# Routing moved within the experts' pipeline, and attention's batches reordered and interleaved

## The chip, the cores and the metric

The kernel runs on one core of one Trainium2 chip. A NeuronCore has TensorE (PE, the matrix engine), VectorE (DVE), ScalarE (ACT), GpSimd (POOL) and SyncE (SP), which mostly issues transfers. Each executes its own instructions in order, and they wait for one another through semaphores. The metric is device time in microseconds of one execution, lower is better.

## The reference

The input is x, 4 batches of 1024 tokens of width 256. Four layers are added to it, each on a layernorm of x: a selective state space layer, an FFN, a linear attention, and the same FFN with the same weights again.

```python
x = x + ssm(layernorm(x))
x = x + ffn(layernorm(x))
x = x + attention(layernorm(x))
x = x + ffn(layernorm(x))

def attention(x):                          # 16 heads of 16, no mask, batches independent
    q, k = relu(x @ Wq) / 4, relu(x @ Wk) / 4
    v, u = x @ Wv, silu(x @ Wu)
    kv  = einsum('bhlk,bhlv->bhkv', k, v)
    out = einsum('bhlk,bhkv->bhlv', q, kv)
    return (srms_norm(out) * u) @ Wo

def ffn(x):
    queries = (x @ W_q).reshape(2, n, 64)   # n = 4096 tokens
    scores  = two top-8 lists against 64 keys each, 64 pair sums, top-8 of these
    ew      = silu(x . down_embed[idx]) * softmax(scores)
    return (silu(x @ gate_w) * (x @ up_w)) @ down_w + sum(ew * up_embed[idx])
```

The first half of the query rows meets the first set of keys and the second half the second, so the routing of tokens of group g needs the queries of group g // 2 and of group g // 2 + 4. A group is 512 tokens; there are 8 groups, two per batch.

## The kernel before

Everything is float32. The tokens are handled in groups of 512 on tiles of 128 partitions.

**State space layer** (`ssm`, lines 112 to 813). It loops over groups and state indices with hand-written order. All its calls go through `Pinned`, which keeps program order. Beside its scan run queues of small stages: `ends` (the layer's output, and a layernorm whose transpose goes to DRAM as `hs[g]`) and `mlps` (the dense half of the first FFN for a group, whose result goes to DRAM as `xs[g]`; `stored` says for which groups). Each stage is announced with its cost in PE time.

**Experts' pipeline** (`experts`, from line 1144 on). When the scan is over, this runs the routed half of the first FFN, still in program order on the pinned engines. The loop has 8 steps per group: `g, k = step // 8, step % 8`. In it:

- `queries` computes qT for two groups in steps k = 0, 1, 2 of odd groups.
- `begin(g + 1)` creates the generator `route` for the next group and runs its first part, eight small matmuls into the one bank named `route`. The rest of `route` is written one part per step by `next(routes[g], None)`: the copy to `r` on ACT, eight times `max` and `max_index` on DVE (tiles `v`, `iu`), the pair sums and their top-8 (`d`, `pv`, `sc`, `left`), counts and normalisation (`cnt`, `zi`, `last`), then `most`, `ex`, the table `tb` on POOL, `code` and `eq`, then `rank`, then a comparison into `eq`, and `tb` multiplied by it. The four DVE operations on 2048 elements (`eq`, `rank`, `eq`, `tb`) take some 2.3 us each.
- `apply(g)` begins at k = 2 and takes 14 steps: four products `emb` with a silu into `wt`, transposes of `tb` into `st` (two banks), the weighing of `wt` by `st` on DVE, the products `up` into `o` (two banks), and the sums `raised` of `x` and `o` on DVE.
- `beside(cost)` lets waiting stages of `ends` and `mlps` run on the PE: `left` is raised by a constant each step, capped at 6.0, and lowered by `COST[k]`, the PE time of the step's own work.

Since the engines are in order, what is written first in a step is also executed first. In a step before the change the part of `route` is written ahead of the parts of `apply`.

**Attention** (`attention`, lines 817 to 937). Here the engines are not pinned: a scheduler of the framework orders the instructions on each engine, from the program order, the dependencies and the buffers. A batch is a pass of `for b in range(B)`: layernorm and transposes of its two groups into `hT`; eight times the products for k, v and gate, evacuated to `kk` (ACT), `vv` (DVE) and `u` (ACT), and the accumulation in two banks `kv`; the query products to `qT` (ACT); the masked `kvb`; eight output products `po`, each copied to `o` (DVE), squared to `sq` (ACT) and reduced to `oss` (DVE); square root (ACT), reciprocal, `u * o` (POOL), the scaling into `o` (DVE); transposes to `oT`, the products with `Wo`, and the sums into `x`. The PSUM pools are `at_mm` (four banks), `at_kv` (two) and `at_o` (two, shared by gate, `po` and `Wo` products). `u` and `o` have one buffer, the other tiles two.

**Last FFN** (`ffn`, lines 1323 to 1371). Layernorm, transposes and queries of the groups in the order 0, 4, 1, 5, 2, 6, 3, 7, then a loop over groups with the routing of the next group beside the dense products. It takes all parts of `route` in one go.

Of the kernel before, what the change touches and what calls it, by code (L numbers as in the profile page):

```python
# [12 lines left out]
F32 = mybir.dt.float32  # L13
# [38 lines left out]
class Net:  # L52
# [764 lines left out]
    def attention(self):  # L817
        nc, tc = self.nc, self.tc
        with ExitStack() as ctx:
            wp = ctx.enter_context(tc.tile_pool(name="at_w", bufs=1, reuse_waits="tile"))  # L820
            one = ctx.enter_context(tc.tile_pool(name="at_one", bufs=1, reuse_waits="tile"))
            two = ctx.enter_context(tc.tile_pool(name="at_two", bufs=2, reuse_waits="tile"))
            mm = ctx.enter_context(tc.tile_pool(name="at_mm", bufs=4, space=PSUM, reuse_waits="tile"))
            kvp = ctx.enter_context(tc.tile_pool(name="at_kv", bufs=1, space=PSUM, reuse_waits="tile"))
# [22 lines left out]
            scale = 1.0 / DH**0.5  # L847
            BT = L // P

            for b in range(B):  # L850
                groups = (2 * b, 2 * b + 1)
                hT = two.tile([P, KD, L], F32, tag="hT", name="hT")
                for i, g in enumerate(groups):
                    ln = two.tile([P, TG, D], F32, tag="ln", name="ln")
                    self.layernorm(g, ln)
                    for k in range(KD):
                        ps = self.transposed(mm, ln, k)
                        nc.vector.tensor_copy(hT[:, k, i * G : (i + 1) * G], ps)
                kv = [
                    kvp.tile([P, P], F32, tag=f"kv{c}", name=f"kv{c}") for c in range(KD)  # L860
                ]
                u = one.tile([P, BT, D], F32, tag="u", name="u")
                for t in range(BT):
                    ts = slice(t * P, (t + 1) * P)
                    ps = self.product(mm, [(hT[:, k, ts], wkv[:, k, :]) for k in range(KD)])
                    kk = two.tile([P, D], F32, tag="kk", name="kk")
                    nc.scalar.activation(kk, ps[:, :D], AF.Relu, scale=scale)
                    vv = two.tile([P, D], F32, tag="vv", name="vv")
                    nc.vector.tensor_copy(vv, ps[:, D:])
                    for c in range(KD):  # L870
                        nc.tensor.matmul(
                            kv[c], lhsT=kk[:, c * P : (c + 1) * P],
                            rhs=vv[:, c * P : (c + 1) * P], start=t == 0, stop=t == BT - 1,
                        )
                    ps = self.product(
                        op, [(hT[:, k, ts], wu[:, k, :]) for k in range(KD)], n=D, tag="o"
                    )
                    nc.scalar.activation(u[:, t, :], ps, AF.Silu)
                qT = two.tile([P, KD, L], F32, tag="qT", name="qT")
                for c in range(KD):  # L880
                    for i in range(L // G):
                        ps = self.product(
                            mm,
                            [
                                (wq[:, k, c * P : (c + 1) * P], hT[:, k, i * G : (i + 1) * G])
                                for k in range(KD)
                            ],
                        )
                        nc.scalar.activation(
                            qT[:, c, i * G : (i + 1) * G], ps, AF.Relu, scale=scale  # L890
                        )
                kvb = two.tile([P, KD, P], F32, tag="kvb", name="kvb")
                for c in range(KD):
                    nc.vector.tensor_tensor(kvb[:, c, :], kv[c], mask, ALU.mult)
                o = one.tile([P, BT, D], F32, tag="o", name="o")
                ss = two.tile([P, BT, HEADS], F32, tag="oss", name="oss")
                for t in range(BT):
                    po = op.tile([P, D], F32, tag="o", name="po")
                    for c in range(KD):
                        nc.tensor.matmul(  # L900
                            po[:, c * P : (c + 1) * P],
                            lhsT=qT[:, c, t * P : (t + 1) * P], rhs=kvb[:, c, :],
                            start=True, stop=True,
                        )
                    nc.vector.tensor_copy(o[:, t, :], po)
                    sq = two.tile([P, D], F32, tag="sq", name="sq")
                    nc.scalar.activation(sq, po, AF.Square, scale=1.0 / DH**0.5)
                    nc.vector.tensor_reduce(
                        ss[:, t, :], sq.rearrange("p (h d) -> p h d", d=DH), AX.X, ALU.add
                    )  # L910

                nc.vector.tensor_scalar(ss, ss, 1e-24, None, ALU.max)
                rt = two.tile([P, BT, HEADS], F32, tag="ort", name="ort")
                nc.scalar.activation(rt, ss, AF.Sqrt)
                nc.vector.reciprocal(ss, rt)
                for t in range(BT):
                    nc.gpsimd.tensor_tensor(u[:, t, :], u[:, t, :], o[:, t, :], ALU.mult)
                    nc.vector.tensor_tensor(
                        o[:, t, :].rearrange("p (h d) -> p h d", d=DH),
                        u[:, t, :].rearrange("p (h d) -> p h d", d=DH),  # L920
                        ss[:, t, :].unsqueeze(2).to_broadcast([P, HEADS, DH]),
                        ALU.mult,
                    )
                for i, g in enumerate(groups):
                    oT = two.tile([P, KD, G], F32, tag="oT", name="oT")
                    for k in range(KD):
                        ps = self.transposed(mm, o[:, i * TG : (i + 1) * TG, :], k)
                        nc.scalar.copy(oT[:, k, :], ps)
                    for t in range(TG):
                        ps = self.product(  # L930
                            op,
                            [(oT[:, k, t * P : (t + 1) * P], wo[:, k, :]) for k in range(KD)],
                            n=D, tag="o",
                        )
                        nc.vector.tensor_tensor(
                            self.x[g][:, t, :], self.x[g][:, t, :], ps, ALU.add
                        )


    def expert_weights(self, pool):  # L940
# [27 lines left out]
    def route(self, nc, w, g, qT, pools, got):  # L968
# [21 lines left out]
        v = sm.tile([P, 2 * M4, TOPK], F32, tag="v", name="v")  # L990
        iu = sm.tile([P, 2 * M4, TOPK], U32, tag="iu", name="iu")
        for i in range(2 * M4):
            nc.vector.max(v[:, i, :], r[:, i, :])
            nc.vector.max_index(iu[:, i, :], v[:, i, :], r[:, i, :])
        yield
# [148 lines left out]
    def experts(self, w, xpool, xs, hs, rest):  # L1144
# [3 lines left out]
        with ExitStack() as ctx:  # L1148
# [121 lines left out]
                yield  # L1270

            left = [0.0]
            COST = (0.9, 0.9, 1.7, 3.4, 3.4, 1.7, 1.7, 2.7)

            def beside(cost):
                left[0] = min(left[0] + 3.6, 6.0) - cost
                for q in (ends, mlps):
                    c = q.next_cost()
                    if c is not None and c[0] <= left[0]:
                        q.stage()  # L1280
                        left[0] -= c[0]
# [5 lines left out]
            for _ in range(3):  # L1287
                next(asked)
                beside(1.7)
            begin(0)  # L1290
            load(hT, 0)
            applied = []
            for step in range(8 * NG + 6):
                g, k = step // 8, step % 8
                if k == 0 and g < NG:
                    while g not in rest.stored:
                        ends.stage()
                        mlps.stage()
                    self.x[g] = xpool.tile([P, TG, D], F32, tag=f"x{g}", name=f"x{g}")
                    nc.sync.dma_start(out=self.x[g], in_=xs[g])  # L1300
                if g < NG:
                    next(routes[g], None)
                if k == 2 and g < NG:
                    applied.append(apply(g))
                for a in list(applied):
                    if next(a, self) is self:
                        applied.remove(a)
                if g + 1 < NG:
                    if k == 0 and g % 2:
                        asked = queries((g + 1) // 2)  # L1310
                    if k < 3 and g % 2:
                        next(asked)
                    if k == 7:
                        begin(g + 1)

                    if k == 5 and g % 2 == 0 and g + 2 < NG:
                        load(asks, (g + 2) // 2)
                        load(asks, (g + 2) // 2 + half)
                    if k == 6:
                        load(hT, g + 1)  # L1320
                beside(COST[k] + (1.7 if g % 2 and k < 2 else 0))

# [120 lines left out]
```

## Time and profile before

| what | value |
|---|---|
| median of 3 runs | 2202.4 us (2200.65 to 2205.84) |
| the profiled execution | 2205.35 us, span 2203.6 us |
| TensorE | 1923.9 us busy (87%), mean granted clock 0.951 |
| VectorE | 1591.7 us busy (72%) |
| ScalarE, GpSimd | 1020.0 us (46%), 1029.5 us (47%) |
| experts' pipeline | about 1204 to 1473 us |
| attention | about 1473 to 1697 us |
| last FFN | about 1697 us to the end |

Busy time is the union of an engine's instructions. A line L47 stands for everything that goes through `Pinned`, and L106 for all products made by the helper `product`, so such work is told apart by its tiles: `out<-in` names what is written and read. In a timeline a row begins with its start and its length in us, and ends in brackets with the time that the engine stood idle before it and what ended that. One matmul of the program in float32 shows as two or more rows of the profile.

### The profile page before, as it was taken

How to read it: one execution, taken by the hardware profiler on the slowest of the kernel's cores; microseconds unless marked ns; L12 is line 12 of the kernel's file. 1: busy time of each engine (PE TensorE's matmuls, PEld its weight loads, DVE VectorE, ACT ScalarE, POOL GpSimd, SP SyncE). 2: the span in 40 equal slices, each digit the busy share in tenths (PEclk: the TensorE clock that was granted, in tenths of full speed). 3: DMA queues.
4: the chain of work that ended last, by engine and by line, in shares of the span. 5: the costliest groups of instructions: out<-in, count | busy, mean ns of one | idle time of the engine just before them, and what ended most of it. 6: DMA issues, size and time to landing. Idle time of an engine off the chain costs nothing.

```text
span 2203.6 us, 22814 instructions
## 1 busy us (share of the span) xinstructions
PE 1923.9 (87%) x7712; PEld 1215.5 (55%) x7712; DVE 1591.7 (72%) x2843; ACT 1020.0 (46%) x1557; POOL 1029.5 (47%) x691
## 2 busy tenths in 40 slices
PE   6586888989889899799878898878888899999999
PEld 2334545656556556456554555556665466666665
DVE  2798988969989889798897888874445555555551
ACT  2465686766767767767645242213332311111111
POOL 2559778687787877878875214211111000000000
PEclk9797999999999999999989999989999999999999
DMA  2311212222122221222113032020000000000000
GB/s 72 97 54 39 68 51 75 62 81 70 62 78 58 71 77 61 82 72 63 53 60 117 19 115 77 29 82 0 1 0 1 1 10 10 10 10 10 10 9 11
DMA packets 84757, 106.13 MB, mean 48 GB/s; under 512 B 7840, under 2 KB 53920, under 8 KB 84640
## 3 DMA queue, kind: packets, MB, share of 16 engines
q1 hardware_dynamic: 78064, 98.00, 14.4%
q10 hardware_dynamic: 6576, 6.67, 0.9%
q8 instruction: 61, 1.00, 0.2%
q14 instruction: 56, 0.46, 0.1%
HBM read 90.75 MB, written 13.89 MB: 47 GB/s over the span
## 4 chain that ended last, share of the span: by engine, by line
PE 56%; DVE 20%; ACT 11%; issue 6%; POOL 4%; DMA 2%; ACTq 0%; SPq 0%; DVEq 0%; POOLq 0%
PE ps L106 22%; PE hT L47 5%; DVE h L47 4%; PE conv L47 4%; DVE acc L47 4%; PE gate L47 3%; PE up L47 3%; ACT L47 3%; ACT a L47 3%; PE xin L47 2%; PE down L47 2%; PE out L47 2%; PE emb L47 2%; PE dt L47 2%; PE o L47 2%
## 5 line engine op out<-in xcount | busy, mean ns | idle before, releaser
L47 POOL TENSOR_TENSOR u<-dx,bt 128x1024 f32<-128x1024 f32 x256 | 603.7, 2366 | 264.9 <-DVE h L47 133.7
L47 PE MATMUL hT<-ident,h 128*128 128x128 f32 x2048 | 305.6, 290 | 120.3 <-DVE acc L47 118.0
L47 DVE SCALAR_TENSOR_TENSOR acc<-hT,cT,acc 128x512 f32<-128x512 f32 x512 | 355.8, 736 | 40.6 <-PE hT L47 39.7
L47 ACT ACTIVATE a<-delta,a_neg 128x512 f32<-128x512 f32 x512 | 340.1, 688 | 92.1 <-DVE h L47 72.0
L47 PEld LDWEIGHTS hT<-ident,h 128*128 128x128 f32 x2048 | 247.2, 148 | 245.3 <-DVE acc L47 194.3
L47 DVE TENSOR_TENSOR_SCAN h<-a,state,u 128x512 f32<-128x512 f32 x256 | 314.9, 1267 | 38.6 <-ACT a L47 37.5
L47 DVE TENSOR_TENSOR_SCAN h<-a,u 128x512 f32<-128x512 f32 x256 | 299.4, 1206 | 59.3 <-ACT a L47 54.6
L1068 POOL TENSOR_TENSOR tb<-ex,d 128x2048 f32<-128x2048 f32 x8 | 29.1, 3641 | 400.8 <-PE ps L106 370.3
L1365 DVE TENSOR_TENSOR act<-s,ps 128x512 f32<-128x512 f32 x64 | 43.8, 685 | 145.3 <-PE ps L106 145.3
L1363 ACT ACTIVATE s<-ps 128x512 f32<-128x512 f32 x64 | 38.2, 597 | 229.5 <-PE ps L106 222.3
L47 ACT ACT_TABLE_LOAD x92 | 118.0, 1283 | 45.8 <-DVE d L47 22.9
L47 PE MATMUL up<-hT,up_w 128*128 128x512 f32 x256 | 123.8, 609 | 7.7 <-DMA up_w<-in_up_w 6.5
L47 PE MATMUL down<-w_down_w,av 128*128 128x256 f32 x512 | 121.2, 382 | 9.3 <-DVE xw L47 7.9
L47 PE MATMUL gate<-hT,gate_w 128*128 128x512 f32 x256 | 122.3, 610 | 5.5 <-DMA gate_w<-in_gate_w 5.5
L106 PE MATMUL ps<-hT,w_gate_w 128*128 128x512 f32 x256 | 121.5, 597 | 4.3 <-DVE act L1365 4.3
L106 PE MATMUL ps<-hT,w_up_w 128*128 128x512 f32 x256 | 120.9, 595 | 0.0
L106 PE MATMUL ps<-w_down_w,act 128*128 128x256 f32 x512 | 116.6, 380 | 3.9 <-DVE x L1140 3.9
L47 POOL TENSOR_TENSOR tb<-ex,d 128x2048 f32<-128x2048 f32 x8 | 45.9, 5742 | 145.6 <-DVE code L47 145.6
L47 PEld LDWEIGHTS down<-w_down_w,av 128*128 128x128 f32 x512 | 95.4, 191 | 32.0 <-issue 9.7
L106 PEld LDWEIGHTS ps<-w_down_w,act 128*128 128x128 f32 x512 | 96.0, 190 | 22.1 <-DVE x L1140 9.7
L47 PE MATMUL conv<-xin,taps 128*128 128x512 f32 x224 | 104.8, 595 | 1.5 <-ACT xc L47 1.5
L47 POOL TENSOR_TENSOR av<-av,up_v 128x512 f32<-128x512 f32 x64 | 82.4, 1291 | 14.2 <-ACT up_v L47 14.2
(250 smaller groups left out, 3280.8 us busy)
## 6 DMA issues: line engine op xcount, KB each, us to landing
bt<-bcd SPq DMA_DIRECT2D x128, 256.0 KB, 3.3
gate_w<-in_gate_w SPq DMA_DIRECT2D x64, 128.0 KB, 3.0
up_w<-in_up_w SPq DMA_DIRECT2D x64, 128.0 KB, 2.5
hT<-hs SPq DMA_DIRECT2D x16, 512.0 KB, 4.3
taps<-conv_d SPq DMA_DIRECT2D x28, 256.0 KB, 3.7
xw<-in_x SPq DMA_DIRECT2D x8, 512.0 KB, 4.4
in_wT<-in_in_wT SPq DMA_DIRECT2D x8, 512.0 KB, 4.6
skip_wT<-in_skip_wT SPq DMA_DIRECT2D x8, 512.0 KB, 4.7
```

The lines of the kernel that those rows point to most:

```text
L47: return self.tc.keep_in_program_order(f(*args, **kw))
L106: self.nc.tensor.matmul(ps, lhsT=lhsT, rhs=rhs, start=i == 0, stop=i == len(pairs) - 1)
L1068: nc.gpsimd.tensor_tensor(tbv, ex.unsqueeze(3).to_broadcast(sht), d[:, M4:, 0:NKEY].unsqueeze(2).to_broadcast(sht), ALU.mult,)
L1363: nc.scalar.activation(s, pg, AF.Silu)
L1365: nc.vector.tensor_tensor(a, s, pu, ALU.mult)
```

## The change

In the experts' pipeline:

- In a step, the part of the next group's routing is now written after the parts of `apply`, so behind its sums and weighings.
- `begin(g + 1)` moves from k = 7 to k = 5, and at k = 6 the next part, the copy to `r`, is written as well. For group 0 both are written ahead of the loop.
- The eight `max` and `max_index` are split by a further `yield` into four and four, at k = 0 and k = 1. The later parts keep their steps.
- `COST` exchanges its entries for k = 5 and k = 7, and `left` is raised by 3.5 in place of 3.6 per step.

In attention the body of the loop becomes the generator `batch(b)` with two `yield`s: ahead of the masked `kvb`, and after the last `oss`. The batches are taken in the order 0, 2, 1, 3. The output part of a batch (up to `oss`) is written first, then the first part of the next batch (up to `qT`), then the last part of the former (norm, gating, `Wo`, sums). `u` and `o` get two buffers and the pool `at_one` goes.

`route` is shared with the last FFN, which takes all its parts at once; the further `yield` changes nothing there.

```diff
@@ attention
-            one = ctx.enter_context(tc.tile_pool(name="at_one", bufs=1, reuse_waits="tile"))
...
-            for b in range(B):
+            def batch(b):
                 groups = (2 * b, 2 * b + 1)
...
-                u = one.tile([P, BT, D], F32, tag="u", name="u")
+                u = two.tile([P, BT, D], F32, tag="u", name="u")
...
+                yield
                 kvb = two.tile([P, KD, P], F32, tag="kvb", name="kvb")
...
-                o = one.tile([P, BT, D], F32, tag="o", name="o")
+                o = two.tile([P, BT, D], F32, tag="o", name="o")
...
+                yield
 
                 nc.vector.tensor_scalar(ss, ss, 1e-24, None, ALU.max)
...
+            order = [batch(b) for b in (0, 2, 1, 3)]
+            next(order[0])
+            for i, now in enumerate(order):
+                next(now)
+                if i + 1 < B:
+                    next(order[i + 1])
+                next(now, None)
@@ route
         for i in range(2 * M4):
+            if i == M4:
+                yield
             nc.vector.max(v[:, i, :], r[:, i, :])
             nc.vector.max_index(iu[:, i, :], v[:, i, :], r[:, i, :])
@@ experts
-            COST = (0.9, 0.9, 1.7, 3.4, 3.4, 1.7, 1.7, 2.7)
+            COST = (0.9, 0.9, 1.7, 3.4, 3.4, 2.7, 1.7, 1.7)
 
             def beside(cost):
-                left[0] = min(left[0] + 3.6, 6.0) - cost
+                left[0] = min(left[0] + 3.5, 6.0) - cost
...
             begin(0)
+            next(routes[0])
             load(hT, 0)
...
-                if g < NG:
-                    next(routes[g], None)
                 if k == 2 and g < NG:
                     applied.append(apply(g))
                 for a in list(applied):
                     if next(a, self) is self:
                         applied.remove(a)
+                if g < NG:
+                    next(routes[g], None)
...
-                    if k == 7:
+                    if k == 5:
                         begin(g + 1)
+                    if k == 6:
+                        next(routes[g + 1])
```

## The prediction

> **What bounds the kernel now.** I read the page first for the stages, then busy time by stretches, then the waits of TensorE (PE) and VectorE (DVE) in the two stages the diff touches, then the timeline around the longest of them.
>
> The page (40 slices of 55 us): DVE is at 6 to 9 tenths up to about 1487 us and at 4 or 5 after it; the PE clock row has an 8 in the slice from 1432 to 1487 us, where the PE pauses.
>
> ```profile
> span 2203.6 us, 22814 instructions
> ...
> DVE  2798988969989889798897888874445555555551
> ...
> PEclk9797999999999999999989999989999999999999
> ```
>
> Busy time of three stretches (columns: length, then busy time with instruction counts for PE, PE weight loads, DVE, ACT, POOL, then PE clock, DMA share, GB/s): experts' pipeline, attention, last FFN.
>
> ```profile
> 1200.00:1472.00 272.00, 230.87 (x866) 152.59 (x866) 221.38 (x644) 70.22 (x99) 70.78 (x33) 0.94 0.21 72
> 1472.00:1697.00 225.00, 199.04 (x837) 135.78 (x835) 102.36 (x281) 65.63 (x139) 28.78 (x39) 0.93 0.03 9
> 1697.00:2204.00 507.00, 490.50 (x1696) 300.98 (x1696) 257.44 (x677) 98.70 (x145) 33.35 (x12) 1.00 0.03 9
> ```
>
> In the experts' stage PE and DVE are both some 80% busy: neither is the bound alone, each waits for the other. In attention only the PE is loaded. The last FFN is PE work at full clock, and its order hardly changes.
>
> Who waits in the experts' stage from its first top-8 on (columns: total us, times, longest):
>
> ```profile
> PE o L47 <- DVE x L47: 21.1, 7, 5.0
> PE st L47 <- DVE wt L47: 12.0, 7, 4.2
> ...
> DVE v L47 <- ACT r L47: 14.8, 5, 4.3
> DVE xw L47 <- PE down L47: 9.6, 4, 5.0
> DVE x L47 <- PE o L47: 7.7, 8, 1.5
> ```
>
> The timeline shows why:
>
> ```profile
> 1419.29 2.29 DVE L47 TENSOR_TENSOR eq<-iota,code 128x2048 f32<-128x2048 f32 x1
> ...
> 1421.50 0.74 DVE L47 TENSOR_TENSOR x<-x,o 128x256 f32<-128x256 f32 x2
> 1421.96 5.72 PE L47 MATMUL o<-w_up_emb,wt 128*128 128x256 f32 x16 [5.02 <-DVE x L47]
> ```
>
> The PE's third output product needs one of the two `o` banks, which the sum `x` frees. The sum takes 0.42 us, but on DVE it stands behind the next group's routing, `eq` last. After the 5.02 us gap 16 matmuls take 5.72 us instead of 3.6.
>
> In attention, per batch:
>
> ```profile
> 1519.90 2.33 PE L97 MATMUL tr<-ident,o 128*128 128x128 f32 x9 [4.13 <-DVE o L918]
> ...
> 1522.06 5.17 PE L106 MATMUL ps<-w_Wo,oT 128*128 128x256 f32 x16
> ```
>
> The PE idles 4.13 us through norm, square root and gating of a batch, then runs slowly.
>
> **What the Trainium skill says.** "TensorE: Matmul & The Clock Gate", Part 1: a PE idle for about 3.4 us falls to half clock and needs about as long busy to return. The trace agrees: after 5.02 us idle 16 matmuls lose 2.1 us, and clocks of 0.83 and 0.87 stand in the two most broken group stretches. "Perfetto Trace Analysis", Identifying Performance Opportunities: where the most contended engine changes between regimes, interleave them. It fits: attention's projections leave DVE idle, its output part leaves the PE idle. "ScalarE: Activation LUTs", What ACT_TABLE_LOAD costs: 1283 ns per load and about 1380 ns of drain. The trace shows loads of 1.28 us; the drain has no row of its own.
>
> **The change, part by part.** All savings are from the profiled execution, 2205.35 us (span 2203.6), which is 2.95 above the median of 2202.4; I subtract savings from the median.
>
> *Attention.* Instructions are the same, apart from order and doubled `u` and `o`. A batch repeats every 54.75 us (1530.31 to 1585.06). Its PE work at gapless rates: key/value/gate loop 8 x 3.03 = 24.2 (steps at 1546.58, 1549.60), query products 16 x 0.43 = 6.9, `po` 32 x 0.108 = 3.4, two sets of 16 transposes at 0.11 = 3.5, `Wo` 32 x 0.215 = 6.9. Sum 44.9, so 9.9 us a batch is lost: 4.1 for `o`, 1.6 for `sq` (four gaps of about 0.5 between `po` pairs), 2.8 slow clock (9 transposes 2.33 against 1.0; 16 `Wo` 5.17 against 3.7), 1.4 in small ones. The changed program's PE order puts the next batch's LN transposes and first projections between `po` pairs, and the previous batch's `Wo` after the next batch's query products. So three of the four losses go; the last batch's output part has nothing beside it and keeps its own.
>
> What stays: I laid the new order out with the durations above. `po` pairs still wait for copy (0.42) plus square (0.42) of the pair before, with 5 and 10 transposes (0.55, 1.1) between: about 1.6 us a transition with the `vv` copies now behind `ln` and `oss` on DVE. Each moved `Wo` block waits for two 0.59 us ACT copies behind the last `qT` copy, twice: 1.6. In the later transitions `po`, `Wo` and the gate products share two banks: 0.9 more each. Kept: 3 x 1.6 + 3 x 1.6 + 2 x 0.9 = 11.4. Saved 29.7 - 11.4 = **18 us** (12 to 25). The two table loads (2 x 1.28, or 5.3 with the skill's drain) now stand in the next batch's loop: `kk` and `u` behind them are late by 3 to 5 us once; four `mm` banks cover the first. I take 0 and keep 6 us over three batches as the bad end, and below zero nothing, since ACT gains no idle time here.
>
> *Experts: routing behind the sums, and begun at k = 5.* DVE work is unchanged; `r` now exists two steps ahead of its top-8. Measured by groups (first top-8 to the next; the last to the last sum): 24.65, 34.50, 31.36, 31.16, 33.28, 32.93, 29.75, 38.97, together 256.6. The busier of PE and DVE in each: 22.97, 29.05, 27.55, 28.70, 30.52, 30.86, 25.76, 34.14, together 229.6. The rest, 27 us or 3.4 a group, is mutual waiting. In the changed order I count PE products and DVE operations by group at the same durations: busier engine 23.0, 29.3, 26.3, 28.3, 26.6, 28.4, 28.6, 31.2, together 221.7. The 8 us come from the PE pieces of the MLPs being spread later (rate 3.5 for 3.6: the last `down` products now lie beside group 6's weighing), and 3 us of `ln` moved out of the tail.
>
> Waiting does not vanish: `v<-r` goes (14.8 less the 3.25 of the first), and of `o<-x` and `st<-wt` I expect half, as sums and weighings now precede the long routing operations, but sums wait for `up` products that stand behind MLP pieces. I take 2.2 a group, 17.6: stage 239.3, **17 us** less. Ends: 3.4 a group gives 8, 1 a group gives 27.
>
> Moved steps on other queues: the routing's 8 small matmuls (0.9 us) go two steps earlier on PE, ahead of two `emb` products; the `r` copy (0.59) precedes two silus on ACT, which idles most of the stage; the POOL table product (5.74) keeps its step; on SP the loads of `hs` and `x` keep their number, and the `gate_w`/`up_w` loads move by a step. I cost these at nothing: ACT (70 of 272) and DMA (0.21) hide them.
>
> *Junction.* The first `ln` of attention now follows the last `x` sum on DVE, where before it lay inside the tail. Four `ln` (0.34 each), four transposes and two `hT` copies (0.69) put the first projection 3.5 to 4 us after the last sum; before it was 3.4 (1473.42 to 1476.81), because it waited for the `Wv` load (2.10). I take 1 us lost (0 to 3).
>
> Sum: 18 + 17 - 1 = 34; 2205.35 - 34 = 2171 for a profiled run, **2168 us** against the median.
>
> **Rivals.**
> 1. Only attention gains: the sums now wait for PE products, so mutual waiting stays above 4 us a group and eats the regrouping. 2202 - 18 = 2184. For it: `x<-o` already waits 8 times; against: those are short, 1.5 at most.
> 2. Both nearly ideal: waits of 1 a group, attention keeps 5 instead of 11. 27 + 25 - 1 = 51, 2151. Against: two `op` banks and one in-order DVE.
> 3. Only the experts' stage gains: the doubled tiles and new order stall on ACT's table loads and `Wo` copies, returning the 18. 2202 - 16 = 2186. Against: ACT is busy 66 of 225 there.
> 4. Slower: DVE blocks at the sums. At k = 4 `raised` waits on DVE for two `up` products, and the whole routing queues behind it, then the table, then the next group's transposes. The wait is the PE's time from weighing to sum (`emb` 1.7, `up` 3.4, plus MLP pieces of 1.7 each) less DVE's cover (3.5 + 3.9 for top-8 and counts). It is zero up to one piece and 1.7 for each more; cancelling 34 us over 8 groups needs 4.3 us more a group, three pieces beyond that one. The budget (3.5 a step, capped at 6.0, less the step's own work) leaves about two. With four pieces: 8 x 5.1 + 3 = 44 lost against 34 gained, 2212.
> 5. The change doesn't do what it says, since attention's order is a scheduler's: the built order shows it moved, so only a few per cent.
>
> **How the numbers follow.** Likeliest 0.62 at 2168 (own range 2158 to 2178); rival 1 0.13; rival 3 0.08; rival 2 0.10; rivals 4 and 5 0.07, split 0.05 slower and 0.02 within. The 80% range, 2150 to 2190, takes in rivals 1 to 3 and the bounds above. A measurement can tell about 0.2% (4.4 us) from no change: faster 0.92 (the first four less 0.01 for their edges), same 0.03, slower 0.05.
>
> **What would show it.** Right: `v<-r` gone from DVE's waits; `o<-x` on PE at half or less; group spacing of the table products near 29; the 4.13 us waits before `tr<-ident,o` only once, in the last batch; attention near 207 us; the last FFN at 507. Wrong: new DVE waits `x<-o` above 2 us, PE waits on `u` or `kk` after a table load, or an experts' stage above 265.

## The result, and the profile after

The changed kernel took 2167.52 us in the median of six runs (2166.62 to 2179.4), the kernel before 2203.03 (2200.06 to 2205.84) beside it: a ratio of 0.9847, 95% interval 0.9822 to 0.9873. The forecast was 2168. The profiled execution took 2167.88 us.

Executions of one kernel lie up to 18 us apart (of the six here four lie near 2167 and two near 2178), and most of that is there when the scan ends, before any changed instruction (its last `acc` ended between 1198.2 and 1214.8 us in the traces below); so stages are compared from there on, and whole times by their ratios.

The page of the changed kernel: span, busy tenths of VectorE, and the PE's clock. DVE's heavy part ends in the same slice as before, the 27th, but a slice is now 54.2 us long in place of 55.1, so that it ends at about 1462 us in place of 1487. The 8 in the clock row, in the tail of the experts' stage, is still there.

```profile
span 2166.2 us, 22802 instructions
...
DVE  2798998978989979888798789984446545555551
...
PEclk9798999999999999999999999989999999999999
```

Busy time by stretches of the changed kernel (length, then PE, weight loads, DVE, ACT, POOL with counts, PE clock, DMA share, GB/s): experts' stage, attention, last FFN.

```profile
1200.00:1459.00 259.00, 228.19 (x864) 152.27 (x864) 223.29 (x628) 70.53 (x99) 71.45 (x31) 0.93 0.24 79
1459.00:1658.20 199.20, 190.32 (x832) 129.03 (x833) 101.15 (x298) 64.67 (x139) 30.92 (x40) 0.98 0.02 5
1658.20:2166.20 508.00, 492.04 (x1696) 301.73 (x1696) 257.17 (x676) 98.69 (x145) 33.33 (x12) 0.99 0.03 9
```

DVE's busy time is within 2 us of what it was in each stretch, and so is the PE's in the last FFN. In attention the PE is busy 8.7 us less (190.32 for 199.04), with its clock at 0.98 in place of 0.93, and idle 9 us in place of 26. In the experts' stage it is busy 2.7 us less, and the clock is no better (0.93 for 0.94): what shrank there is idle time.

The changed kernel's waits of PE, then of DVE, from the end of the scan to the last experts' sum (total us, times, longest):

```profile
PE st L47 <- DVE bnmv L83: 6.9, 1, 6.9
PE o L47 <- DVE x L47: 6.3, 3, 3.2
...
PE st L47 <- DVE wt L47: 3.5, 3, 1.7
```

```profile
DVE x L47 <- PE o L47: 12.8, 9, 4.1
DVE v L47 <- ACT r L47: 11.4, 1, 11.4
```

The waits for `x` and `wt` fell to a third, and `v<-r` is left only ahead of the first top-8. Others grew: the sums wait longer for `o` (12.8 us for 8.5, each in nine waits; the 7.7 of the prediction leaves out the last one), the PE waits 3.6 us for a `gate_w` transfer where it was 0.7, and it stands still for 6.9 us once, at a wait put down to `bnmv`, a layernorm statistic of attention. What stands still there are the transposes `st`, which read the table `tb`:

```profile
1417.90 1.94 PE L47 MATMUL st<-ident,tb 128*128 128x128 f32 x8 [6.90 <-DVE bnmv L83]
```

The last long operation on `tb` ended at 1417.76 us on DVE, and the statistic, 0.17 us long, stands directly behind it. So this is a wait for the table, under the name of its neighbour.

In attention, PE's waits in the changed kernel:

```profile
PE tr L97 <- DVE o L919: 4.1, 1, 4.1
PE tr L97 <- DVE ln L88: 1.9, 2, 1.1
...
PE po L900 <- ACT sq L907: 0.4, 2, 0.2
PE ps L106 <- ACT oT L929: 0.2, 1, 0.2
```

Its timeline where one batch gives way to the next (start, length, and idle time in brackets where there was any):

```profile
1573.59 4.88 PE L106 MATMUL ps<-hT,w_Wq 128*128 128x512 f32 x11
1578.31 1.25 PE L97 MATMUL tr<-ident,o 128*128 128x128 f32 x10
1579.63 1.99 PE L106 MATMUL ps<-w_Wo,oT 128*128 128x256 f32 x8
1581.46 0.38 PE L97 MATMUL tr<-ident,o 128*128 128x128 f32 x2
```

No row has a bracket: query products of the next batch, then ten transposes of `o` in 1.25 us where nine took 2.33, and `Wo` blocks at 1.99 for eight. The last batches repeat every 45.97 us, counted between their query products, in place of 54.75, with the PE busy for 45.90 of them.

Where the 36.6 us between the two traces came from. The columns are lengths in us, each from the border before: from the end of the scan to the first top-8, from there to the experts' last sum `x`, from there to the last FFN's first query products `w_W_q`, from there to the end; the total is their sum.

| kernel | ratio to before (95%) | to first top-8 | to last sum | to first `w_W_q` | to the end | total |
|---|---|---|---|---|---|---|
| before | 1 | 13.18 | 256.63 | 226.00 | 504.18 | 999.99 |
| changed | 0.9847 (0.9822 to 0.9873) | 11.45 | 244.65 | 201.42 | 505.86 | 963.38 |
| attn_noil | 0.9991 (0.9970 to 1.0013) | 13.13 | 256.76 | 225.94 | 504.37 | 1000.20 |
| attn_only | 0.9892 (0.9859 to 0.9925) | 13.09 | 256.69 | 201.40 | 505.71 | 976.89 |
| experts_only | 0.9911 (0.9880 to 0.9942) | 11.40 | 241.67 | 222.47 | 504.27 | 979.81 |
| behind_only | 0.9933 (0.9907 to 0.9959) | 13.01 | 243.96 | 225.12 | 504.20 | 986.29 |
| begin_only | 0.9947 (0.9921 to 0.9972) | 13.31 | 246.84 | 225.35 | 504.23 | 989.73 |
| after_r36 | 0.9844 (0.9809 to 0.9879) | 13.04 | 243.43 | 201.27 | 505.70 | 963.44 |
| after_inorder | 0.9834 (0.9800 to 0.9867) | 11.49 | 241.02 | 201.76 | 505.75 | 960.02 |
| after_exlate | 0.9819 (0.9794 to 0.9844) | 11.50 | 245.24 | 201.10 | 507.40 | 965.24 |
| after_tail | 0.9813 (0.9784 to 0.9843) | 11.33 | 244.64 | 193.15 | 504.07 | 953.19 |
| after_again | 0.9852 (0.9826 to 0.9878) | 11.37 | 244.70 | 201.43 | 505.80 | 963.30 |
| inorder_tail | 0.9794 (0.9766 to 0.9823) | 11.32 | 241.62 | 193.33 | 505.42 | 951.69 |
| inorder_tail_r36 | 0.9806 (0.9774 to 0.9838) | 13.20 | 243.34 | 193.45 | 505.25 | 955.24 |

### The profile page after: what moved, and what is told of

Its sections match the earlier page's. It is cut to its first block, busy times and chain, and to the rows that moved or that the text cites. A ratio compares the mean times of both kernels' runs of the same rounds, so it can differ in the third digit from the quotient of the medians.

```text
span 2166.2 us, 22802 instructions
## 1 busy us (share of the span) xinstructions
PE 1914.2 (88%) x7712; PEld 1209.5 (56%) x7712; DVE 1592.9 (74%) x2843; ACT 1019.4 (47%) x1557; POOL 1032.6 (48%) x691
## 4 chain that ended last, share of the span: by engine, by line
PE 57%; DVE 22%; ACT 12%; issue 5%; POOL 3%; DMA 2%; ACTq 0%; SPq 0%; DVEq 0%; POOLq 0%
PE ps L106 23%; PE hT L47 5%; PE gate L47 4%; DVE h L47 4%; PE conv L47 4%; DVE acc L47 4%; PE up L47 3%; ACT L47 3%; ACT a L47 3%; PE xin L47 2%; PE dt L47 2%; PE out L47 2%; PE down L47 2%; DVE eq L47 1%; ACT av L47 1%
## 5 line engine op out<-in xcount | busy, mean ns | idle before, releaser
L47 POOL TENSOR_TENSOR av<-av,up_v 128x512 f32<-128x512 f32 x64 | 87.7, 1374 | 12.0 <-ACT up_v L47 12.0
```

Source lines behind the costliest of these rows:

```text
L47: return self.tc.keep_in_program_order(f(*args, **kw))
```

## The experiments

### The two parts alone

attn_only is the kernel before with the diff's attention part, experts_only the changed kernel with the old attention.

```diff
 # attn_only, from the kernel before; experts_only is the reverse, from the changed one
-            for b in range(B):
+            def batch(b):
...
+            order = [batch(b) for b in (0, 2, 1, 3)]
```

> The kernel before with attention's part of the change alone (generators, order 0, 2, 1, 3, doubled u and o); the experts' pipeline as before. Theory: the changed kernel's trace takes 24.6 us less from the experts' last sum to the end of attention and 1.7 more in the last FFN, and this is attention's own doing: 2203 - 23 = 2180 (2176 to 2184), batches 46 us apart, one 4.1 us wait before the o transposes. Rival: part of it came from the experts' stage ending differently (layernorms and statistics placed elsewhere), then the saving is under 17 us: 2187 or more.

> The changed kernel with attention as before, so the experts' part alone. Theory: the stage gains 14.5 us as in the changed kernel (12.0 from its first top-8 to its last sum, 2.5 from an earlier first top-8): 2203 - 14.5 = 2188.5. Rival: attention's new batch order costs the experts' stage time in the changed kernel, because the layernorm statistics of groups 2 and 3 fall into group 6's routing on the VectorE (30.4 us busy there against 25.8 before, and one 6.9 us wait of the PE for st behind bnmv); then without it the stage gains 20 or more: 2183 or less, and this wait is gone.

By the totals attention alone saves 23.1 us, as expected, and the experts' part alone 20.2, between its expectation (14.5) and what its rival would make of the stage (20 or more; it gained 16.7 with the earlier first top-8). The rival's cause is there, its size is not. That is 43.3, and the whole change saves 36.6. The lost 6.7 us lie mainly in two columns. The experts' stage is 3.0 us longer with the new attention behind it (244.65 for 241.67). And the experts' part alone shortens the old attention by 3.5 us; about 1.9 of them at its entry, up to the first `kv` (6.65 us after the last sum for 8.59), where the wait for the `Wv` transfer falls from 2.10 to 1.18 us and four products take 1.96 in place of 3.33. The other 1.6 lie in somewhat shorter periods of the old batches; why was not settled. The new attention has no such wait and no such periods, so that this gain can't come twice.

By the rival the wait of 6.9 us was to be gone. It is halved: the same transposes wait 3.24 us in experts_only, here under the name of `tb`. (A wait of 0.8 us on `bnmv` is left in group 4, at another place.)

```profile
PE st L47 <- DVE tb L47: 8.4, 4, 3.2
PE o L47 <- DVE x L47: 6.4, 3, 3.5
```

```profile
1412.14 1.06 PE L47 MATMUL st<-ident,tb 128*128 128x128 f32 x8 [3.24 <-DVE tb L47]
```

### The experts' part taken in two

behind_only writes the routing behind the sums and does nothing else; begin_only begins it at k = 5, with the copy at k = 6 (both ahead of the loop for group 0), the split and the exchanged costs, but leaves it ahead of the sums and the constant at 3.6.

```diff
 # behind_only
-                if g < NG:
-                    next(routes[g], None)
                 if k == 2 and g < NG:
...
+                if g < NG:
+                    next(routes[g], None)
 # begin_only
...
-                    if k == 7:
+                    if k == 5:
                         begin(g + 1)
+                    if k == 6:
+                        next(routes[g + 1])
```

> The kernel before with one edit: the routing's part of a step is written behind apply's parts. begin stays at k = 7, the copy to r at k = 0, no split of the top-8, the rate 3.6. Theory of the prediction: sums and weighings no longer stand behind routing, so the PE's waits o<-x (21.1 us) and st<-wt (12.0) fall to less than half, but the VectorE still waits for r: some 8 to 10 us gained, 2194. Rival: the early beginning is what cuts the loop; the order alone gains under 3 us, since the VectorE carries the same work: 2201.

> The kernel before with begin at k = 5, the copy to r at k = 6, the split of the top-8 and the exchanged costs, but the routing still ahead of the sums and the rate 3.6. Theory of the prediction: the VectorE's wait v<-r (14.8 us) goes, and the chain from a group's emb products over its route products to the next top-8 is cut: 5 to 7 us gained, 2197, with the PE's waits o<-x still near 20 us. Rival: the sums behind the routing still set the pace, nothing is gained: 2203.

The stage shrinks by 12.7 us in the one and by 9.8 in the other, by 15.0 with both (experts_only, with the constant at 3.5): each alone gets most of it. Counted by groups as in the prediction, the mutual waiting falls from 27.1 us to 15.6 in behind_only, and to 21.8 in begin_only. The totals fall by 13.7 and 10.3 us, more than the 8 to 10 and 5 to 7 that were expected. Both end `v<-r` but for the first (3.3 us); for behind_only that was not expected, since it does not begin any earlier. They differ in what is left on the PE's side: the wait `o<-x` in behind_only, where it was to fall to less than half, then in begin_only, 21.1 in the kernel before:

```profile
PE o L47 <- DVE x L47: 14.2, 4, 6.5
```

```profile
PE o L47 <- DVE x L47: 19.0, 5, 5.8
```

Only the two together bring it to 6.4, and the constant is not needed for that (5.9 in after_r36, below). The sums wait 7.5 and 7.8 us for `o` in these two, less than the 8.5 of before, but 9.8 in experts_only. The split and the exchanged costs were not run apart.

### Order of the batches without interleaving

The kernel before, with the new order and second buffers for `u` and `o`, but each batch in one piece.

```diff
-            for b in range(B):
+            def batch(b):
...
+            for b in (0, 2, 1, 3):
+                for _ in batch(b):
+                    pass
```

> The kernel before, with the batches of attention in the order 0, 2, 1, 3 and with doubled u and o, but every batch written in one piece, not interleaved. Theory (the gain of attention comes from the next batch's projections standing between a batch's output products): the order and the second buffers bring nothing by themselves, the 4.1 us waits before the transposes of o return in all four batches and the batch period stays near 54 us; the time is within 4 us of the kernel before, a ratio of 0.998 to 1.002. Rival (the second u and o alone let the engines overlap batches, since PE and ACT may run ahead): half of attention's gain or more, 10 us and over, a ratio below 0.995, period below 51 us.

The ratio holds 1, the totals differ by 0.2 us, and PE's waits in attention are those of before:

```profile
PE tr L97 <- DVE o L919: 16.5, 4, 4.1
PE po L900 <- ACT sq L907: 6.3, 12, 0.6
```

So it is the interleaving that makes attention's gain. Order and second buffers bring nothing without it. The order is not needed with it either (after_inorder, below: 201.76 us for 201.42); interleaving without the second buffers was not run.

### The rate

```diff
-                left[0] = min(left[0] + 3.5, 6.0) - cost
+                left[0] = min(left[0] + 3.6, 6.0) - cost
```

> The changed kernel with left raised by 3.6 a step, as before the change, in place of 3.5. Theory (the rate only adjusts for the exchanged costs, the edits of order make the gain): stage of 243 to 247 us, the time within 3 us of the changed kernel, 2165 to 2171. Rival (the smaller rate is what keeps MLP pieces from standing between a weighing and its sum): the waits of VectorE for o, 12.8 us in the changed kernel, rise above 20, the stage exceeds 250 us and the time is 6 us or more above the changed kernel, 2174 or more.

The total is the same (963.44 for 963.38), with parts that cancel: the first top-8 comes 1.6 us later after the scan, and the stage is 1.2 us shorter. The rival is excluded: the sums wait 7.4 us for `o`, less than the 12.8 with 3.5. The 1.7 us by which the changed kernel reaches its first top-8 sooner belong to the constant (11.3 to 11.5 us in all traces with 3.5, 13.0 to 13.3 in all with 3.6).

### The statistics in the routing of group 6

```diff
-            order = [batch(b) for b in (0, 2, 1, 3)]
+            order = [batch(b) for b in (0, 1, 2, 3)]
```

> The changed kernel with the batches in the order 0, 1, 2, 3, interleaved as before. Theory (the order 0, 2, 1, 3 defers the layernorm statistics of groups 2 and 3 on VectorE into the routing of groups 6 and 7, where the PE then waits 6.9 us for st and the clock falls to 0.79): in the old order these statistics stand behind the sums of their groups, the 6.9 us wait goes, the stage from the first top-8 to the last sum falls from 244.7 to about 241.7 us as with the old attention behind it, and the kernel takes 3 to 4 us less than the changed one, about 2164. Attention stays at 199 to 200 us. Rival (the statistics cost the same VectorE time wherever they stand, and the tail's slow clock comes from the end of the work): stage 244 to 246, time the same as that of the changed kernel within 2 us. Second rival (the last FFN begins with groups 0 and 4, so their batches must be first): the FFN starts later and the kernel is 2 to 5 us slower than the changed one.

The stage fell to 241.02, the total by 3.4 us, as the theory had it. The wait of 6.9 us did not go, though: `st` waits 3.24 us there, as in experts_only. The last FFN's first query products come 0.3 us later after the last sum, which excludes the second rival's 2 to 5. Whole times can't show 3 us here (intervals 0.9800 to 0.9867 and 0.9822 to 0.9873). By groups (busy time as above), the last two of the changed kernel:

```profile
1386.93:1418.14 31.21, 23.19 (x103) 17.02 (x102) 30.42 (x83) 6.22 (x8) 4.35 (x2) 0.95 0.16 51
1418.14:1458.92 40.78, 32.45 (x112) 23.35 (x111) 32.50 (x93) 5.64 (x7) 7.58 (x5) 0.79 0.26 88
```

and the last two of after_inorder, where the PE's clock is 1.00 and 0.87:

```profile
1400.78:1428.26 27.48, 23.34 (x103) 17.10 (x101) 26.49 (x76) 6.61 (x9) 5.73 (x1) 1.00 0.18 58
1428.26:1467.19 38.93, 29.51 (x112) 21.73 (x112) 31.32 (x86) 5.64 (x7) 10.54 (x4) 0.87 0.28 92
```

DVE lost 3.9 us of busy time in group 6, more than the seven small instructions that left it can take (0.17 to 0.42 each). DVE's timeline in the changed kernel tells where the rest was:

```profile
1403.77 0.18 DVE L47 SCALAR_TENSOR_TENSOR code<-fi,steps 128x32 f32<-128x32 f32 x1
1403.87 0.42 DVE L82 BATCH_NORM_STATS2 bnst<-x 128x6 f32<-128x256 f32 x1
1404.20 5.58 DVE L47 TENSOR_TENSOR eq<-iota,code 128x2048 f32<-128x2048 f32 x1
```

and GpSimd's beside it:

```profile
1404.02 3.62 POOL L47 TENSOR_TENSOR tb<-ex,d 128x2048 f32<-128x2048 f32 x1 [16.36 <-DVE code L47]
```

In the other groups `eq` starts first, takes 2.29 us, and GpSimd's product shows 5.73 to 5.76. Here a deferred statistic came in between: the product started 0.18 us ahead of `eq`, took 3.62, and `eq` ended 2.14 us after it. The two don't run side by side. The Trainium skill says so, in "SBUF — State Buffer", Who interferes with whom: a VectorE instruction with two inputs in SBUF contends with a GpSimd instruction that reads SBUF, and "Issue order, not op shape, decides who blocks." The trace agrees, both ways: with `eq` first the product is the longer by 2.1 us, with the product first `eq` by 3.3.

### The product behind eq

In the changed kernel `ex` and the product, which stood ahead of `code`, go behind the first `eq`; the statistic stays where it is.

```diff
-        nc.vector.tensor_tensor(ex, ...)
-        nc.gpsimd.tensor_tensor(tbv, ...)
         code = sm.tile([P, M4, TOPK], F32, tag="code", name="code")
...
         nc.vector.tensor_tensor(eq, ...)
+        nc.vector.tensor_tensor(ex, ...)
+        nc.gpsimd.tensor_tensor(tbv, ...)
```

> The changed kernel with the small operation ex, which releases GpSimd's table product tb, and that product written directly behind the first long eq in place of ahead of code; the statistics stay where they are, one of them between code and eq in group 6. In the changed kernel's group 6 this one statistic let the product begin 0.18 us before eq, and eq took 5.58 us in place of 2.29, while the product took 3.62 in place of 5.74. Theory (these two operations do not run side by side: whichever comes first makes the other wait, and the 3.3 us that eq waits there are the statistics' price): eq takes 2.29 us in all eight groups, the product about 3.6 in all of them from the end of eq on, the PE's 6.9 us wait falls to about 3.5, and the stage from first top-8 to last sum falls from 244.7 to 241 to 242 us. Rival (the deferred statistics cost by their own VectorE time, and the long eq only fills time in which VectorE would have waited anyway): stage of 243.5 to 245, the waits of VectorE for o grow by what eq loses. Second rival (the product, begun later, now runs into the second eq and the product of tb and eq): those take 3 us and more, and the stage is longer than 246.

The mechanism came out as expected, its yield did not. From the tile view of the experts' stage (shortest, median and longest ns of each operation), first of the changed kernel, then of this one:

```profile
L47 DVE TENSOR_TENSOR eq<-iota,code x8: 2291/2292/5580, 1227.6 to 1435.0; 128x2048 f32<-128x2048 f32 x8
...
L47 DVE TENSOR_TENSOR eq<-rank,most x8: 2268/2274/3272, 1232.3 to 1442.4; 128x2048 f32<-128x2048 f32 x8
```

```profile
L47 DVE TENSOR_TENSOR eq<-iota,code x8: 2277/2292/2293, 1226.8 to 1436.5; 128x2048 f32<-128x2048 f32 x8
...
L47 DVE TENSOR_TENSOR eq<-rank,most x8: 2273/2669/3658, 1231.5 to 1442.7; 128x2048 f32<-128x2048 f32 x8
```

The first `eq` takes 2.29 us in all eight groups. Group 6 fell from 31.21 to 28.48 us and the 6.9 us wait to 4.2: of the 3.7 us that the order of batches saves in group 6, at least 2.7 are this block (0.6 us of its gain went to a longer second `eq` there), and at most 1 the statistics themselves. But the later product now meets the second `eq` (median 2.67), and groups 1 and 3 are 3.2 and 1.5 us longer, so that the stage is 0.6 longer than the changed kernel's. The second rival had named this meeting, though not its size. All eight second `eq` together are only 1.8 us longer; what else holds group 1 was not settled. The edit lies in `route`, which the last FFN uses too, and that takes 507.40 us for 505.86. (The ratio of the whole times is the better one, 0.9819 for 0.9847, but the intervals overlap.)

### The last batch's norm covered

```diff
             for i, now in enumerate(order):
-                next(now)
                 if i + 1 < B:
+                    next(now)
                     next(order[i + 1])
+                if i + 2 == B:
+                    next(order[i + 1])
                 next(now, None)
```

> The changed kernel with one more exchange in attention: the output part of the last batch is written ahead of the last part of the batch before it, so that eight Wo blocks and sixteen transposes stand between the last po and the transposes of the last o. Theory: the 4.13 us wait before the last batch's transposes of o goes and with it its slow clock (transposes 2.33 in place of 1.0, Wo 5.69 in place of 4.0), while the last FFN's slow start (1.7 us) stays; 5 to 7 us less than the changed kernel, about 2161.5, attention at about 193.5 us. Rival (the last batch's norm waits on ACT and DVE behind the copies and sums of the batch before, so the wait only moves behind the Wo blocks): 0 to 2 us less. Second rival: po products wait for banks that the Wo blocks hold, and the time is the same or 2 us more.

It saves 10.2 us by the totals, more than expected: 8.3 in attention, and 1.8 in the last FFN, whose slow start was to stay (1.98 us for its first four query products in place of 3.38). The wait of 4.13 us is gone; in its place the PE waits 0.38 and 0.55 us for `sq` and 0.38 for a sum `x`. PE's timeline of after_tail behind that, with one gap, at the border:

```profile
1655.59 0.60 PE L97 MATMUL tr<-ident,o 128*128 128x128 f32 x4
1656.03 4.05 PE L106 MATMUL ps<-w_Wo,oT 128*128 128x256 f32 x16
1661.01 1.32 PE L97 MATMUL tr<-ident,ln 128*128 128x128 f32 x8 [0.93 <-DVE ln L88]
```

### Both edits together

> The changed kernel once more, unaltered, as the base for the two versions beside it on the same chip. Theory (the differences of some 11 us between executions of one kernel arise in the scan ahead of every changed instruction): counted from the end of the last scan operation to the end the span is 963.4 us within 1 us, whatever the whole time is; stage of the experts 244.7, from the last sum to the first query products of the last FFN 201.4. Rival (the differences arise in the changed stages): these lengths move by more than 3 us with the whole time.

> The changed kernel with both edits in attention: batches in the order 0, 1, 2, 3, and the output part of the last batch written ahead of the last part of the batch before it. Theory (the two losses are separate: statistics that stand in the routing of groups 6 and 7, and the last batch's uncovered norm): stage of 241.0 us as with the order alone, 193.2 us from the last sum to the first query products as with the exchange alone, 504 us of last FFN, so 951.5 us from the end of the scan, 12 us less than the changed kernel. Rival (one takes up the other's gain, as the last Wo blocks delay the sums that the statistics of the last FFN need): 955 or more, no better than the exchange alone.

> As the version with both edits in attention, with left raised by 3.6 a step in place of 3.5. Theory (in the changed kernel 3.6 took 1.2 us off the stage, and in the old order of batches its groups 6 and 7 lose their wait for statistics as well): stage of about 240 us, 1 us less than with 3.5, and 950.5 from the end of the scan. Rival (with 3.6 the second group takes 32.7 in place of 29.9 us, and without the statistics nothing in the later groups pays for it): stage of 242 to 244, 1 to 3 us more than with 3.5.

The changed kernel itself: 963.30 us from the end of the scan for 963.38 in its first trace, while the scan ended 4.3 us sooner. So the scatter lies ahead of the change. With both edits the total is 951.69, 11.6 less than the changed kernel beside it. The expected 951.5 is met by chance, since the stages that were named with it give only 949.6, with 11.4 to the first top-8: the two gains do not quite add up (3.4 and 10.2 alone), as the stage is 0.6 us and the last FFN 1.4 us longer than each alone had it. In whole times it is 2161.17 us (2156.28 to 2167.83) for 2177.11 (2163.53 to 2177.81), the ratios to the kernel before 0.9794 (0.9766 to 0.9823) and 0.9852 (0.9826 to 0.9878). This is the shortest version run. With 3.6 in addition the rival was right: the stage is 1.7 us longer (group 1 takes 32.69 us for 29.85), the first top-8 comes 1.9 later.

## Why the prediction was right, and where it wasn't

**The sum.** Predicted 18 + 17 - 1 = 34 us; by the stages it was 1.7 to the first top-8, 12.0 in the experts' stage, 24.6 in attention, and 1.7 lost in the last FFN, together 36.6. The total is near because two errors have opposite signs: behind the last sum 17 us were forecast (18 less 1 at the junction) and 24.6 came, in the experts' stage 17 were forecast and 12.0 came. The mechanisms were right in the main, their sizes not, and that the sum came out is luck; so is the median within 0.5 us of 2168, since six further runs of the same kernel have a median of 2177.11 at nearly the same ratio (0.9852).

**Attention, mis-sized.** Three of four losses went, as said: attn_noil shows that it was the interleaving, and the 4.13 us wait stands once, in the last batch. The term that failed is the 11.4 us that the new order was to keep: the wait of `po` for `sq` is 0.4 us in all, that of `Wo` for `oT` 0.2, and none for shared banks is to be seen. What the layout by hand missed is that the scheduler puts two and four transposes between `Wo` blocks, so that the copies run beside a block of the other half. A period is 1.1 us over the 44.9 of its gapless sum, not 3.8, and attention's stretch is 199.2 us, not 207. The table loads cost the PE nothing, as taken, and the drain that the prediction allowed for is not to be seen: in the kernel before `sq` ended at 1516.71, the load ran from 1516.73 to 1518.01, and the next instruction of ACT began at 1518.02.

**Experts, mis-sized the other way.** Predicted 239.3, measured 244.65. The waiting was right: 2.2 a group was taken, and the lengths of the groups less the busier engine leave 16.8, or 2.1; the table products are 29.6 us apart, near the 29 that was named. The busier engine was wrong: 221.7 taken, 227.8 measured, counted in the same way. In after_inorder it is 223.6, so that the order of the batches is 4.2 of the 6.1 us; where the other 1.9 come from was not settled. The constant, to which the prediction put most of the fall of the busier engine, is worth 0.7 us of it in the changed kernel (228.5 in after_r36), and 3.4 with both edits in attention (223.8 for 227.2). The step that failed counted instructions at their durations of before, and the list of moved instructions held `ln` but not attention's statistics, which the order 0, 2, 1, 3 of another part of the diff brought into groups 6 and 7. There one of them changed which of `eq` and GpSimd's product came first.

**Costed at nothing.** The moved `r` copies, silus and loads: in the main rightly. PE's waits on ACT are 1.2 and 0.8 us, no longer than before, and the one that grew is for the `gate_w` transfer, whose move by a step the prediction had named and costed at nothing: 3.6 us in group 2 for 0.7. The constant 3.5 was counted in the regrouping only; that it brings the first top-8 sooner was not foreseen.

**Junction and FFN.** One us was taken as lost. At the first accumulation `kv` nothing is (8.69 us after the last sum for 8.60): the first products start 0.7 later, and four of them take 1.88 us in place of 3.33. The last FFN took 508.0 in its stretch, 1 over the forecast: after the last batch's end, with its wait of 4.13 us, its first four products take 3.38 us for 1.98, and after_tail, which removes that wait, has 1.98 again.

**The rivals.** attn_only and experts_only exclude rivals 1 and 3: both parts gain. Rival 2 was right by half: attention came to its 25 us, while the waiting in the experts' stage stayed at 2.1 us a group, not 1. Rival 4's mechanism is there, in small: `x<-o` reached 4.1 us, above the 2 that was to speak for it, but its total grew by 4.3 us over eight groups, where it needed 34. Rival 5 is excluded by attn_noil and attn_only, between which only the interleaving differs.

## What to carry to other kernels

Where an engine stands idle in one part of a loop and its partner in another, interleaving the parts of successive passes can give nearly all of it back, as it did in attention (9 us idle in place of 26); then look at the last pass, which has no successor, and let the pass before it wait instead (10 us here). A wait carries the name of the instruction that ended last: before a wait is called gone, look for it under other names. A change of order reaches the instructions that a scheduler places elsewhere: list what moved on every engine, small statistics too. Before believing that two order edits add up, run each alone; they gave 12.7 and 9.8 us here, and 15.0 together.

## What the runs showed of the hardware that was not expected

The order of arrival decides which of two blocked instructions pays. A 0.42 us statistic ahead of `eq` let GpSimd's product start first: that took 2.1 us less (3.62 for 5.74), and `eq` 3.3 us more (5.58 for 2.29). VectorE never waited for GpSimd in this stage, so that the product's waiting had cost it nothing. Such a wait counts as busy time of the blocked instruction and stands in no list of waits; it shows only when the durations of like operations are held beside each other. The same block is in the last FFN, of the kernel before too: the product starts 1.07 us ahead of the second `eq` in seven of eight groups, and that takes 4.72 us there in place of 2.27. VectorE is busy for only half of that stretch.

And the scan stage ended up to 16.6 us apart in the traces (1198.2 to 1214.8) with the stages behind it repeating to 0.1 us: where the scan ended at 1202.8, 1198.5 and 1214.0 us (after, after_again, after_tail), the experts' stage took 244.65, 244.70 and 244.64. So a stage's length in one trace told here what the medians of six whole times could not.
